# One attention kernel: inner products and values handed to partition groups from SBUF, a new order of the first stages, and the last chunk of keys computed with the values

## The chip, the cores and the metric

The kernel runs on one core of a Trainium2 chip. The metric is the device time in microseconds of one execution. Three executions of the kernel before took 497.56, 498.48 and 500.09 us; their median is 498.48 us. One more execution was profiled: it took 498.01 us, of which the traced span is 496.2 us.

## The reference, cut to what matters

For each of 8 batches, 112 queries of 320 channels (20 heads of 16) attend to 375 tokens of 512 numbers. The last 4 tokens are image prompts, the other 371 are text. Everything is float32.

```python
q   = heads(x @ W_q)                     # 20 heads of 16
k_t = heads(text @ W_k); v_t = heads(text @ W_v)
probs_t  = softmax(q @ k_t.T * D**-0.5)
text_out = probs_t @ v_t
k_ip = heads(ip @ W_k_ip); v_ip = heads(ip @ W_v_ip)
qsem = l2norm(probs_t @ text)            # per head, over 512 numbers
sem  = qsem @ l2norm(ip).T
probs_ip = softmax(q @ k_ip.T * D**-0.5 + 0.5 * sem) * mask
out = (text_out + probs_ip @ v_ip) @ W_out + b_out + x
```

The norm of `qsem` is p G p' for a row p of probabilities, where G holds the inner products of all tokens with each other. So the kernel multiplies the probabilities by G and not by the tokens: one product with the 371 x 371 matrix (only its upper half, doubled off the diagonal), the 4 prompt columns, a column of ones (the softmax's sum) and the head's 16 value columns gives everything that a head needs.

## The kernel before, in words

**Tiling.** Tokens are cut into three chunks of 128 (NT = 3) and into twelve blocks of 32 (BLK = 12, four blocks q to a chunk). Embedding channels are four chunks of 128. The 320 channels of queries and keys are two full chunks and a last one of 64, which is spread over 128 partitions with zeros between the heads (`spread`, L116), so that each head of a group stands at the start of 32 partitions. Heads are handled in five groups g of four heads a; head a of a group uses partitions 32a to 32a+31, and TensorE's four row groups work on four heads.

**Work per batch b.** `transposed_context` (L331) brings the tokens into `ctxT` with the embedding on partitions. `gram` (L352) makes the inner products, and ScalarE and GpSimd write them, doubled off the diagonal, to `ug`. `gram_to_dram` (L374) writes `ug` to the DRAM tile `ud`, and `gram_to_groups` (L378) reads it into `u`, once for each of the four partition groups a, so that token block q of every chunk lies on the 32 partitions of each a. `values` (L403) makes the values in `vext`; `values_to_dram` (L419) and `values_to_groups` (L425) take them through `vd` into `vr` in the same manner. `placed` (L441) copies 16 columns of a head from `vr` into `u` on GpSimd before each group. `keys` (L388) makes the keys `kT`, `project_queries` (L269) the queries of two batches at a time.

**Work per group.** `scores` (L467) makes a head's 112 x 371 scores; `probabilities` (L485) takes the negative row maximum on VectorE (`nmx`), the exponential on ScalarE (`p`), and sends p by one transfer a head on SP's queue into `xg`. `transposed` (L500) is one VectorE transpose of 32 x 32 blocks for the whole group, `xg` to `xgT`. `multiplied` (L510) is the product of `xgT` with `u`, twelve blocks j times four heads. `reduced` (L533) copies the value part (`pvs`) and multiplies and sums the rest with p (`junk`, `ss`). `finish` (L551) computes the prompt attention from these sums and the output product `ps_o`.

**What sets the order.** TensorE, SyncE and VectorE run the order of the source (`manual_schedule`, L89); in the first stages, up to `prologue.close()` (L742), all engines do. The main loop (L744) goes over 40 steps (b, g). In a step, the scores of the step two later are emitted after blocks j = 0 (heads 0 and 1) and j = 4 (heads 2 and 3), and the VectorE transpose of the next step after j = 2. After a step, `between` (L665) places the next batch's preparation: inner products after g = 0, two chunks of values after g = 1, the last chunk and the first keys after g = 2, the other two chunks of keys after g = 3, and after g = 4 the transposes of the context of the batch after it and, for every other batch, the query projection in one piece. SP issues transfers in the order of the source and stops at one whose data is not ready[...].

**Buffers.** PSUM has four banks for products (`ps_qd`), two for scores (`ps_sc`, also used as spares) and two for the rest (`ps_mm`); `bank` (L80) hands out the latter two kinds.

Of the kernel before, what the change touches and what calls it, by code (L numbers as in the profile page):

```python
# [14 lines left out]
NIP = 4  # L15
# [5 lines left out]
def kernel(  # L21
# [26 lines left out]
    CP = NC * P  # L48
    RG = 32
# [12 lines left out]
    OFF = [QN * sum(WC[:c]) for c in range(NT)]  # L62
    UCOL = QN * sum(WC)
    GCOL = [sum(UV - k * P for k in range(c)) for c in range(NT + 1)]
# [32 lines left out]
    wv_sb = const.tile([P, NE, C], F32, tag="wv_sb", name="wv_sb")  # L97
# [8 lines left out]
    FULL = C // P  # L106
    REST = C - FULL * P

# [26 lines left out]
    nc.scalar.dma_start(x_sb[:, 0, :], x[0])  # L135
    load_channels(nc.scalar, wq_sb, w_q)
# [3 lines left out]
    load_embed(nc.sync, wv_in, w_v)  # L140
    load_embed(nc.sync, wk_sb, w_k)

# [23 lines left out]
    for c in range(NT):  # L166
        nc.gpsimd.memset(ug[:, GCOL[c + 1] - 1 : GCOL[c + 1]], 1.0)

# [11 lines left out]

    def more_constants():
        nc.gpsimd.memset(wo_sb[REST:, FULL, :], 0.0)
        for at in attn_ring:
            nc.gpsimd.memset(at[:, C:], 0.0)
# [6 lines left out]
    def order_values():  # L191

        wv_by = wv_sb.rearrange("p e (a g d) -> p e a g d", g=NG, d=D)
        for i in range(FULL):
            nc.vector.tensor_copy(
                wv_by[:, :, :, 2 * i : 2 * i + 2, :],
                wv_in[:, :, i * P : (i + 1) * P].rearrange("p e (a r d) -> p e a r d", r=2, d=D),
            )
        nc.vector.tensor_copy(
            wv_by[:, :, :, 2 * FULL, :],  # L200
            wv_in[:, :, FULL * P :].rearrange("p e (a d) -> p e a d", d=D),
        )
# [29 lines left out]
    def prompt_projections():  # L232

        for i in range(NC):
            ps = bank(f"ps_kip{i}")
            for e in range(NE):
                nc.tensor.matmul(  # L237
                    ps[:, :N],
                    wkip_sb[:, e, i * P : (i + 1) * P],
                    ipT[:, e, :],  # L240
                    start=(e == 0),
                    stop=(e == NE - 1),
                )
            kip = work.tile([P, N], F32, tag="kip", name=f"kip_{i}")
            nc.scalar.copy(kip, ps[:, :N])
            nc.vector.tensor_tensor(
                kipb[:, i],
                kip.rearrange("p (b n) -> p b n", n=NIP).unsqueeze(2).to_broadcast([P, B, HC, NIP]),
                hmask.unsqueeze(1).unsqueeze(3).to_broadcast([P, B, HC, NIP]),
                ALU.mult,  # L250
            )
            yield
# [16 lines left out]
    def project_queries(bs):  # L269
# [7 lines left out]
        for i in range(NC):  # L277
            cn = min(P, C - i * P)
            ps = bank(f"ps_x_{bs[0]}_{i}", spare=bs[0] > 1 and i == 0)
# [31 lines left out]
    def begin(b):  # L311
# [4 lines left out]
        s["ud"] = dram.tile([P, GCOL[NT]], F32, tag="ud", name=f"ud_{b}")  # L316
        s["vext"] = work.tile([P, NT, GROUP, NG, D], F32, tag="vext", name=f"vext_{b}", bufs=1)
        s["vd"] = dram.tile([TP, C], F32, tag="vd", name=f"vd_{b}")
# [7 lines left out]
    def region(b, c):  # L326

        w = WC[c]
        return st[b]["u"][:, OFF[c] : OFF[c] + QN * w].rearrange("p (q w) -> p q w", w=w)

# [20 lines left out]

    def gram(b):  # L352
# [4 lines left out]
        for c in range(NT):  # L357
            t0 = c * P
            k = min(P, TT - t0)
# [9 lines left out]
            g = ug[:, GCOL[c] : GCOL[c] + T - t0]  # L369
            nc.scalar.mul(g, ps[:, : T - t0], 2.0)  # L370
            nc.gpsimd.tensor_tensor(g[:, :k], g[:, :k], half[:, :k], ALU.mult)  # L371
            yield

    def gram_to_dram(b, c0=0, c1=NT):  # L374
        cols = slice(GCOL[c0], GCOL[c1])
        nc.sync.dma_start(st[b]["ud"][:, cols], ug[:, cols])

    def gram_to_groups(b, chunks):  # L378

        s = st[b]  # L380
        for c in chunks:
            for a in range(GROUP):
                nc.sync.dma_start(
                    region(b, c)[a * RG : (a + 1) * RG, :, : UV - c * P],
                    s["ud"][:, GCOL[c] : GCOL[c + 1]].rearrange("(q i) t -> i q t", i=RG),
                )

    def keys(b):  # L388
        s = st[b]
        for i in range(NC):  # L390
            ps = bank(f"ps_k_{b}_{i}")
            for e in range(NE):
# [10 lines left out]
    def values(b):  # L403
        s = st[b]
        ctxT, vext = s["ctxT"], s["vext"]
        for c in range(NT):
            ps = bank(f"ps_v_{b}_{c}")
            for e in range(NE):
                nc.tensor.matmul(  # L409
                    ps[:, :C],  # L410
                    ctxT[:, e, c * P : (c + 1) * P],
                    wv_sb[:, e, :],
# [3 lines left out]
            nc.scalar.copy(vext[:, c].rearrange("p a g d -> p (a g d)"), ps[:, :C])  # L416
            yield

    def values_to_dram(b, eng):  # L419
        eng.dma_start(  # L420
            st[b]["vd"].rearrange("(c p) x -> p c x", p=P),
            st[b]["vext"].rearrange("p c a g d -> p c (a g d)"),
        )

    def values_to_groups(b, eng):  # L425
        s = st[b]
        w = NG * D
        for a in range(GROUP):
            eng.dma_start(
                s["vr"][a * RG : (a + 1) * RG].rearrange("p j g d -> p j (g d)"),  # L430
                s["vd"][:, a * w : (a + 1) * w].rearrange("(j i) x -> i j x", i=RG),
            )
# [118 lines left out]
    def finish(b, heads=(0, H), eng=None, late=False):  # L551
# [7 lines left out]
        def sm(name):  # L559
            return small.tile([S, H], F32, tag=name, name=f"{name}_{b}_{h0}", bufs=2)[:, :n]  # L560

        def sm4(name):
            return small.tile([S, H, NIP], F32, tag=name, name=f"{name}_{b}_{h0}", bufs=2)[:, :n]
# [54 lines left out]
        ps = bank(f"ps_a_{b}_{h0}")  # L618
# [13 lines left out]
        for i in range(i0, i1):  # L632
            nc.tensor.matmul(  # L633
                ps[:S, :C], aT[:, i, :], wo_sb[:, i, :], start=(i == 0), stop=(i == NC - 1)
            )
        if h1 < H:
# [28 lines left out]
    def between(b, g):  # L665
# [4 lines left out]
        if g == 0:  # L670
            if b == 0:
                run(("pp",), None)
            if new:
                run(("g", nb), lambda: gram(nb), 3)
            if b > 0:
# [10 lines left out]
        if g == 3:  # L686
            if new:
                run(("k", nb), None, 2)
            if b > 0:
                run(("f", b - 1), None)  # L690
        if g == 4:
            if nb + 1 < B:
                run(("c", nb + 1), lambda: transposed_context(nb + 1), 3)
            if b > 0:
                run(("f", b - 1), None)
        if b == 0 and g in (1, 2) or b > 0 and g == 4:
            for bs in later:
                run(("q", bs[0]), lambda: project_queries(bs), 3 if b == 0 else 6)
# [3 lines left out]
    products = gram(0)  # L702
    next(prompts)
    next(context)
    next(context)
    next(prompts)
    next(context)
    order_values()
    for c in range(NT):
        next(products)  # L710
        gram_to_dram(0, c, c + 1)
    drain(values(0))
    values_to_dram(0, nc.scalar)
    load_embed(nc.sync, wkip_sb, w_k_ip)
    spread(nc.gpsimd, wq_sb)
    spread(nc.gpsimd, wk_sb)
    drain(project_queries(pairs[0]))
    loaded[1] = load_ctx(1)
    run(("k", 0), lambda: keys(0))
    gram_to_groups(0, range(NT))  # L720
    values_to_groups(0, nc.sync)
# [3 lines left out]
    run(("k", 0), None)  # L725
# [3 lines left out]
    transposed(0, 0)  # L729
    run(("k", 0), None)  # L730
    spread(nc.gpsimd, wkip_sb)
# [5 lines left out]
    nc.sync.dma_start(x_sb[:, 5:, :], x[5:].rearrange("b s c -> s b c"))  # L737
    drain(transposed_context(1))
    run(("pp",), prompt_projections, 3)
    placed(0, 0)  # L740
# [3 lines left out]
    for n, (b, g) in enumerate(steps):  # L744
        coming = steps[n + LEAD] if n + LEAD < len(steps) else None
        for j, _ in enumerate(multiplied(b, g)):
            at = {0: (0, 1), 4: (2, 3)}.get(j, ())
# [11 lines left out]
        if new:  # L759
            if g == 1:  # L760
                gram_to_dram(b + 1)
                load_next(b + 2)
            elif g == 2:
                gram_to_groups(b + 1, (0, 1))
            elif g == 3:
                gram_to_groups(b + 1, (2,))
                values_to_dram(b + 1, nc.sync)
# [5 lines left out]
        if g == 3 and new:  # L773
            values_to_groups(b + 1, nc.sync)
# [51 lines left out]
```

## Time and profile before

| | |
|---|---|
| median of three runs | 498.48 us (497.56 to 500.09) |
| profiled execution | 498.01 us, span 496.2 us |
| TensorE matmuls busy | 468.3 us, 94% of the span |
| VectorE busy | 321.1 us, 65% |
| ScalarE busy | 180.1 us, 36% |
| GpSimd busy | 105.9 us, 21% |
| mean granted TensorE clock | 0.972 |
| bytes moved by transfers | 67.24 MB, mean 136 GB/s |

An engine's busy time counts only its own work, not its waits[...]. The chain of work that ended last is followed back from the end: at each step to what released an instruction, or to the instruction ahead of it on its engine. In all views PE is TensorE, PEld its weight loads, DVE VectorE, ACT ScalarE, POOL GpSimd, SP SyncE; SPq is the issue of a transfer on SP's queue. A name such as `u<-ud` reads: written from.

### The profile page before, as it was taken

To read this page: it belongs to the slowest core of one execution; us is meant where nothing else is said; L and a number is where in the kernel's file an instruction comes from. 1 tells how busy PE (TensorE), PEld (TensorE's weight loads), DVE (VectorE), ACT (ScalarE), POOL (GpSimd) and SP (SyncE) were. 2 spreads that over 40 slices of the span, in tenths; PEclk is the share of its full clock that TensorE was granted. 3 is DMA by queue.
4 is the path that set the end of the run, shared out by engine and by line. 5 is a ranking of instruction groups with operands and counts; after the bars stand their busy time and mean duration, and the time that the engine had idled before them with its cause. 6 is when DMAs were issued, how large, how long until landed. Compare 5 with 4: busy or idle time off the path is not lost.

```text
span 496.2 us, 12853 instructions
## 1 busy us (share of the span) xinstructions
PE 468.3 (94%) x5106; PEld 361.8 (73%) x5106; DVE 321.1 (65%) x692; ACT 180.1 (36%) x505; POOL 105.9 (21%) x245
## 2 busy tenths in 40 slices
PE   6999999999999999999999999999999999987963
PEld 3657777788777787788778787788777887766751
DVE  3045456687765775687756776687756776678862
ACT  2253232235334352335324342335324432243232
POOL 4301200002501124012501124012501232011540
PEclk9997999999999999999999999999999999998895
DMA  7588447542595236942595236842595227732300
GB/s 217 157 198 237 100 152 163 156 114 63 154 228 153 58 95 172 210 121 67 163 229 142 67 98 171 199 116 76 171 220 140 67 87 162 195 101 78 101 13 12
DMA packets 61075, 67.24 MB, mean 136 GB/s; under 512 B 22128, under 2 KB 56192, under 8 KB 61016
## 3 DMA queue, kind: packets, MB, share of 16 engines
q1 hardware_dynamic: 60096, 65.32, 50.3%
q10 hardware_dynamic: 920, 1.11, 0.8%
q8 instruction: 40, 0.66, 0.6%
q14 instruction: 19, 0.16, 0.1%
HBM read 31.65 MB, written 8.17 MB: 80 GB/s over the span
## 4 chain that ended last, share of the span: by engine, by line
PE 84%; DVE 5%; ACT 3%; DMA 2%; POOL 2%; issue 2%; SPq 1%; POOLq 0%; ACTq 0%; DVEq 0%
PE ps_qd L523 37%; PE ps_k L393 11%; PE ps_v L409 11%; PE ps_g L362 9%; PE ps_s L476 7%; PE ps_q L289 2%; PE ps_c L339 2%; PE ps_o L633 2%; DVE junk L538 1%; POOL wv L606 1%; DMA vr<-vd 1%; DVE qm L298 1%; PE ps_kip L237 1%; PE ps_ip L456 1%; DMA ip_sb<-in_ctx_dram 1%
## 5 line engine op out<-in xcount | busy, mean ns | idle before, releaser
L523 PE MATMUL ps_qd<-u,xgT 32*112 32x296 f32 (+11 forms) x3840 | 244.4, 365 | 3.5 <-POOL u L445 1.4
L523 PEld LDWEIGHTS ps_qd<-u,xgT 32*112 32x112 f32 x3840 | 196.8, 174 | 33.6 <-issue 7.3
L493 ACT ACTIVATE p<-ps_s,nmx 112x371 f32<-112x371 f32 x160 | 82.3, 568 | 159.8 <-DVE nmx L489 141.6
L489 DVE TENSOR_REDUCE nmx<-ps_s 112x1 f32<-112x371 f32 x160 | 77.4, 528 | 76.0 <-PE ps_s L476 74.7
L504 DVE STREAM_TRANSPOSE xgT<-xg 128x1536 f32<-128x1536 f32 x40 | 118.9, 2971 | 5.2 <-DMA xg<-p 5.2
L538 DVE CUSTOM_DVE_ANT_0 junk<-ps_qd,p 112x371 f32<-112x371 f32 x160 | 87.1, 544 | 45.3 <-ACT pvs L536 28.0
L476 PE MATMUL ps_s<-kT,qm 32*112 32x371 f32 x320 | 75.0, 496 | 2.8 <-ACT p L493 2.2
L445 POOL COPY u<-vr 128x64 f32<-128x64 f32 x120 | 26.6, 238 | 224.8 <-PE ps_qd L523 161.5
L393 PE MATMUL ps_k<-ctxT,wk_sb 128*128 128x371 f32 x192 | 63.6, 480 | 0.0
L409 PE MATMUL ps_v<-wv_sb,ctxT 128*128 128x320 f32 x192 | 55.6, 440 | 0.0
L393 PEld LDWEIGHTS ps_k<-ctxT,wk_sb 128*128 128x128 f32 x192 | 35.7, 190 | 21.7 <-issue 1.1
L476 PEld LDWEIGHTS ps_s<-kT,qm 32*112 32x112 f32 x320 | 36.8, 173 | 15.8 <-ACT kT L400 3.2
L362 PE MATMUL ps_g<-ctxT 128*128 128x375 f32 (+2 forms) x192 | 45.3, 394 | 0.7 <-issue 0.7
L409 PEld LDWEIGHTS ps_v<-wv_sb,ctxT 128*128 128x128 f32 x192 | 35.2, 190 | 13.5
L362 PEld LDWEIGHTS ps_g<-ctxT 128*128 128x128 f32 x192 | 33.4, 197 | 12.3 <-issue 3.8
L400 ACT COPY kT<-ps_k 128x371 f32<-128x371 f32 x24 | 11.3, 469 | 41.4 <-PE ps_k L393 41.3
L606 POOL TENSOR_TENSOR wv<-vip,w 112x1280 f32<-112x1280 f32 (+1 forms) x8 | 19.2, 2404 | 31.8 <-DVE w L604 31.8
L298 DVE TENSOR_SCALAR qm<-ps_q,emask 128x224 f32<-128x224 f32 (+1 forms) x25 | 9.2, 400 | 24.2 <-PE ps_q L289 24.0
L416 ACT COPY vext<-ps_v 128x320 f32<-128x320 f32 x24 | 10.2, 427 | 33.5 <-PE ps_v L409 33.5
L371 POOL TENSOR_TENSOR ug<-ug,half 128x128 f32<-128x128 f32 (+1 forms) x24 | 11.3, 472 | 41.6 <-ACT ug L370 41.6
L536 ACT COPY pvs<-ps_qd 112x21 f32<-112x21 f32 x160 | 16.5, 200 | 6.9 <-PE ps_qd L523 6.9
L289 PE MATMUL ps_q<-xT,wq_sb 128*128 128x224 f32 (+1 forms) x90 | 16.8, 332 | 1.9 <-ACT xT L284 0.9
(95 smaller groups left out, 272.4 us busy)
## 6 DMA issues: line engine op xcount, KB each, us to landing
xg<-p SPq DMA_DIRECT2D x160, 162.3 KB
u<-ud SPq DMA_DIRECT2D x32, 188.0 KB
vip<-vipd SPq DMA_DIRECT2D x8, 560.0 KB
ct<-in_ctx_dram SPq DMA_DIRECT2D x16, 256.0 KB
u<-ud SPq DMA_DIRECT2D x32, 124.0 KB
vr<-vd SPq DMA_DIRECT2D x32, 120.0 KB
vd<-vext SPq DMA_DIRECT2D x7, 480.0 KB
ud<-ug SPq DMA_DIRECT2D x7, 372.0 KB
```

The source lines that it names most:

```text
L289: nc.tensor.matmul(ps[:, : n * S], wq_sb[:, j, i * P : (i + 1) * P], xT[:, j, : n * S], start=(j == 0), stop=(j == NC - 1),)
L362: nc.tensor.matmul(ps[:, : T - t0], ctxT[:, e, t0 : t0 + P], ctxT[:, e, t0:T], start=(e == 0), stop=(e == NE - 1),)
L393: nc.tensor.matmul(ps[:, :TT], wk_sb[:, e, i * P : (i + 1) * P], s["ctxT"][:, e, :TT], start=(e == 0), stop=(e == NE - 1),)
L409: nc.tensor.matmul(ps[:, :C], ctxT[:, e, c * P : (c + 1) * P], wv_sb[:, e, :], start=(e == 0), stop=(e == NE - 1),)
L445: nc.gpsimd.tensor_copy(region(b, c)[:, :, UV - c * P :], s["vr"][:, c * QN : (c + 1) * QN, g, :])
L476: nc.tensor.matmul(ps[:S, :TT], qm[a * RG : (a + 1) * RG, i, r, j * S : (j + 1) * S], s["kT"][a * RG : (a + 1) * RG, i, :], start=True, st ...
L489: nc.vector.tensor_reduce(nmx, ps[:S, :TT], AX.X, ALU.max, negate=True)
L493: nc.scalar.activation(p, ps[:S, :TT], AF.Exp, bias=nmx)
L504: nc.vector.transpose(xT.rearrange("p j (k q) -> p q j k", q=QN), xg.rearrange("p q (j k) -> p q j k", k=RG),)
L523: nc.tensor.matmul(banks[a][:S, j * RG : UW], xT[a * RG : (a + 1) * RG, j, :S], region(b, c)[a * RG : (a + 1) * RG, q, q * RG :], start=(j ...
L538: nc.vector.tensor_tensor_reduce(out=junk, in0=ps[:S, :TT], in1=s["p", g][:, a, :], scale=1.0, scalar=0.0, op0=ALU.mult, op1=ALU.add, accu ...
L606: eng.tensor_tensor(wv, s["vip"][:, :, part], w.rearrange("p h n -> p n h").unsqueeze(3).to_broadcast([S, NIP, n, D]), ALU.mult,)
```

## The change

**First stages.** The queries' input and weights and the second batch's context are loaded on SP's queue right behind the values' weights. Four products of the identity with itself are put ahead of everything (`awake`). The first batch's inner products are made block by block as soon as a chunk of context is transposed (`first_gram`). One chunk of values, the transposes of the queries' input and the other chunks of values follow; the projections of queries stand between the first chunk of keys and the scores; the other two chunks of keys follow the scores of two groups. The prompts' keys and values are projected together after the first group and the second batch's inner products.

**Transfers.** `u` is laid out by token block, and so are the rows of `ug`, with 16 columns of zeros at the end of each chunk. `gram_to_groups` copies 32 rows of `ug` to `u`, for each of four blocks and four partition groups, SBUF to SBUF: 16 transfers a batch, 8 after g = 1 and 8 after g = 2. `values_to_groups` does the same with `vext` and `vr`: 8 transfers after g = 2 behind the last chunk of values, 8 after g = 3. `ud` and `vd` are gone.

**Keys.** From the second batch on, the weights of the last 64 key channels stand behind the values' weights, so a chunk of values has 384 columns. GpSimd copies the key part to `k3` with zeros between heads, and three transposes make the last chunk of keys from it.

**Order between groups.** Scores of heads 2 and 3 come after block j = 6, but in the last batch. The three transposes of a query projection go after g = 3 between the last two chunks of keys, the projections after g = 4 around a last part of the output product, which `finish` now yields before. The context of the batch after next is loaded after g = 0. `ps_a` and two of three `ps_x` use score banks. Small tiles of `finish` have one buffer and not two.

```diff
@@ loads
-    nc.scalar.dma_start(x_sb[:, 0, :], x[0])
-    load_channels(nc.scalar, wq_sb, w_q)
     load_embed(nc.sync, wv_in, w_v)
+    nc.sync.dma_start(x_sb[:, 0, :], x[0])
+    load_channels(nc.sync, wq_sb, w_q)
     load_embed(nc.sync, wk_sb, w_k)
+    loaded[1] = load_ctx(1)
@@ region
-        return st[b]["u"][:, OFF[c] : OFF[c] + QN * w].rearrange("p (q w) -> p q w", w=w)
+        u = st[b]["u"].rearrange("p (q w) -> p q w", w=GW)
+        return u[:, :, GCOL[c] : GCOL[c + 1]]
@@ new
+    def awake(n):
+        ps = bank(f"ps_w_{n}", spare=True)
+        for _ in range(n):
+            nc.tensor.matmul(ps[:, :P], ident, ident, start=True, stop=True)
+    def first_gram():
+        ctxT = st[0]["ctxT"]
+        banks = []
+        for c in range(NT):
+            banks.append(ps_qd.tile([P, 512], F32, tag="qd", name=f"ps_g_0_{c}"))
...
+            c0, c1 = c * P, min(c * P + P, T)
+            for r in range(c + 1):
+                for e in range(NE):
+                    nc.tensor.matmul(banks[r][:, c0 - r * P : c1 - r * P],
+                        ctxT[:, e, r * P : (r + 1) * P], ctxT[:, e, c0:c1], ...)
+                if c == NT - 1:
+                    doubled(banks[r], r)
+                yield
@@ gram_to_groups
-                    region(b, c)[a * RG : (a + 1) * RG, :, : UV - c * P],
-                    s["ud"][:, GCOL[c] : GCOL[c + 1]].rearrange("(q i) t -> i q t", i=RG),
+                    st[b]["u"][a * RG : (a + 1) * RG, q * GW : (q + 1) * GW],
+                    ug[q * RG : (q + 1) * RG, :],
@@ keys
+            if b > 0 and i == FULL:
+                for c in range(NT):
+                    rows = min(P, TT - c * P)
+                    nc.tensor.transpose(ps[:, c * P : c * P + rows],
+                        s["k3"][:rows, c].rearrange("p a r d -> p (a r d)"), ident[:rows, :rows])
+                nc.scalar.copy(s["kT"][:, i, :], ps[:, :TT])
@@ values
+        w = C if b == 0 else C + REST
...
+            if b > 0 and c == NT - 1:
+                nc.gpsimd.tensor_copy(s["k3"][:, :, :, 0, :],
+                    vext[:, :, C:].rearrange("p c (a d) -> p c a d", d=D))
@@ values_to_groups
+        for q in blocks:
+            for a in range(GROUP):
+                nc.sync.dma_start(by_block[a * RG : (a + 1) * RG, q],
+                    s["vext"][q * RG : (q + 1) * RG, :, a * w : (a + 1) * w])
@@ finish
-        ps = bank(f"ps_a_{b}_{h0}")
+        ps = bank(f"ps_a_{b}_{h0}", spare=b < B - 1)
...
+            if h1 - h0 == H and i == 1:
+                yield
@@ between, g == 3 and g == 4
-                run(("k", nb), None, 2)
+                run(("k", nb), None, 1)
+            for bs in later if b > 0 else ():
+                run(("q", bs[0]), lambda: project_queries(bs), 3)
+            if new:
+                run(("k", nb), None, 1)
...
+                run(("f", b - 1), None, 1)
+            for bs in later if b > 0 else ():
+                run(("q", bs[0]), lambda: project_queries(bs), 2)
+            if b > 0:
                 run(("f", b - 1), None)
+            for bs in later if b > 0 else ():
+                run(("q", bs[0]), lambda: project_queries(bs), 1)
@@ first stages
-    drain(values(0))
-    values_to_dram(0, nc.scalar)
...
-    drain(project_queries(pairs[0]))
-    loaded[1] = load_ctx(1)
+    drain(products)
+    gram_to_groups(0, range(QN))
+    run(("v", 0), lambda: values(0))
+    run(("q", 0), lambda: project_queries(pairs[0]), 3)
+    run(("v", 0), None, 2)
+    values_to_groups(0, (0, 1))
...
+    run(("q", 0), None)
     run(("k", 0), lambda: keys(0))
+    run(("q", 0), None)
...
+    run(("q", 0), None)
+    values_to_groups(0, (2, 3))
...
-    run(("pp",), prompt_projections, 3)
@@ main loop
-            at = {0: (0, 1), 4: (2, 3)}.get(j, ())
+            at = {0: (0, 1), 6 if b < B - 1 else 4: (2, 3)}.get(j, ())
...
-            if g == 1:
-                gram_to_dram(b + 1)
+            if g == 0:
                 load_next(b + 2)
+            elif g == 1:
+                gram_to_groups(b + 1, (0, 1))
             elif g == 2:
-                gram_to_groups(b + 1, (0, 1))
+                gram_to_groups(b + 1, (2, 3))
             elif g == 3:
-                gram_to_groups(b + 1, (2,))
-                values_to_dram(b + 1, nc.sync)
+                values_to_groups(b + 1, (2, 3))
...
-        if g == 3 and new:
-            values_to_groups(b + 1, nc.sync)
+        if g == 2 and new:
+            values_to_groups(b + 1, (0, 1))
```

## The prediction

> **What bounds the kernel now.** I began with the page's busy table and its chain: matmuls fill TensorE for 94% of the span, and 84% of the chain that ended last is TensorE. Time taken off its instructions, or off a wait between them, is time off the end; work elsewhere counts only where TensorE stands still for it.
>
> ```profile
> PE 468.3 (94%) x5106; PEld 361.8 (73%) x5106; DVE 321.1 (65%) x692; ACT 180.1 (36%) x505; POOL 105.9 (21%) x245
> ...
> PE 84%; DVE 5%; ACT 3%; DMA 2%; POOL 2%; issue 2%; SPq 1%; POOLq 0%; ACTq 0%; DVEq 0%
> ```
>
> Busy time hides short waits, since ends of matmuls are modelled. So I went through the chain in order of time. In one batch the chunk of values and the chunk of keys stand there at their real cost:
>
> ```profile
> 77.45 2.35 PE ps_v L409 x8
> 79.80 2.49 PE ps_k L393 x8
> ```
>
> Between two groups of heads where queries are projected, the chain leaves TensorE:
>
> ```profile
> 267.16 1.42 PE ps_c L339 x12
> 268.58 1.62 PE ps_o L633 x6
> 270.19 0.21 PE ps_x L281 x2
> ...
> 270.43 0.60 ACT xT L284 x2
> ...
> 271.07 1.42 PE ps_q L289 x6
> ...
> 272.51 0.82 DVE qm L298 x2
> ...
> 273.36 0.35 ACT qT L301
> ...
> 273.75 1.40 PE ps_q L289 x6
> ```
>
> TensorE stood from 270.40 to 271.07 and from 272.49 to 273.75, 1.93 us, waiting for a PSUM bank. Elsewhere from 60 to 430 us the chain stays on TensorE, but for the last 11 us. Third, the start: the first weighted product stands at 44.20 us, at half the clock (windows of 2 us; columns are matmul busy time, granted clock, DMA share, GB/s):
>
> ```profile
> 40.00:42.00 2.00, 2.00 (x19) 0.93 0.66 192
> 42.00:44.00 2.00, 1.42 (x7) 0.50 0.74 183
> 44.00:46.00 2.00, 1.80 (x12) 0.50 0.79 252
> 46.00:48.00 2.00, 2.00 (x16) 0.50 1.08 340
> ```
>
> Last, the queue of SP, which the change loads (timeline of one batch):
>
> ```profile
> 247.43 3.81 SPq L383 DMA_DIRECT2D u<-ud  x8
> ...
> 263.45 1.85 SPq L429 DMA_DIRECT2D vr<-vd  x4
> ```
>
> A transfer of 32 partitions takes SP 0.475 us to issue; one of xg<-p takes 0.80 (median of its 160).
>
> [...] weight loads of the first 375-column product are 0.62 us apart (10.55, 11.18, 11.80)[...], until 14.3 us; later chunks run at twice that. [...] transposes from 3.7 to 8.5 us brought no fast clock, and the half clock from 42 us follows transposes and 32-column products. [...] 2.49 us for 8x371 is 0.311 each[...]. [...] here the write of vd takes 2.82 us and the reading back 4.35.
>
> **The change, part by part.**
>
> *Keys.* For seven of eight batches the last chunk loses its eight matmuls, 2.49 us. Values get 64 columns more in 24 matmuls[...]. Three transposes come in at 1.42/12 = 0.118 us: 0.35. Net -0.86, times 7: **-6.0**. The copy to k3 on POOL (0.2 to 0.6 us, like u<-vr and ug) stands about ten us ahead of its transposes; ACT's wider copy of vext adds 0.04. Both are covered by TensorE's next group; without that cover, under 1 us a batch.
>
> *Queries.* The input transposes go one step earlier, between the two last chunks of keys; the output product is split so that its last part stands between the second and third projection. By the chain, the waits of three such stages are 1.92 (159 us), 1.93 and 1.41: 5.3. In the new order the bank that the third projection needs is drained under 1.42 + 0.54 us of other matmuls, against 1.17 of draining. ps_a now takes a score bank: 0.1 to 0.2 us may be lost behind ACT's copies. **-4.9**. The first pair (83 us) keeps its 1.24.
>
> *Scores at block 6.* They are emitted later by two blocks, about 1 us. But the maxima of heads 2 and 3 stand behind VectorE's transpose of 2.97 us, which ends later than either place. I take 0; bounds -0.1 to +0.1 a step, 33 steps, -3 to +3.
>
> *Transfers.* Per batch, 12 u + 4 vr + one ud + one vd become 16 + 16 from SBUF. SP: 32 x 0.475 + 20 x 0.80 + some six others = 34 us of 53 to 58. Worst place, counted from the end of group 2's products: the last p transfer ends at 2.1, eight u at 5.9, vip 6.3, eight vr at 10.1. Heads 0 and 1 of the next p, ready from 7.6, wait behind them until 10.1; but heads 2 and 3, ready at 11.7 and 12.3, then go 0.3 late, and only the last counts for the transpose. That starts some 2.5 us into a group, takes 3.0, and is needed 5.9 + 3.0 us after the group's start (its products and the shortest work between groups), so 3.4 us are to spare. Cost 0. The wait of POOL for vr (63.3 us in 7 places) vanishes; it touches TensorE only at 437 us: **-0.3**. The 16 waits on separate u transfers in a batch's first group cost about nothing: 12 such stand there now, and that group takes 6.07 us in the chain (217.06 to 223.13) against 5.86 for the next (228.40 to 234.26).
>
> *Start.* The inner products start as soon as the first chunk is transposed, but with the same 741 columns, cold. Counting half-clock durations (1.7 us per 128-column block of four) from 5.8 us, with the clock rising at 14.3 as now, they end at 16.2, against 17.1. [...] From there: values 6.5, transposes 0.4, query 0.85, keys 2.5, query 0.85 bring the first scores at +11.1 (now +13.75). Exponentials after a 1.28 us table load: +13.9 to +15.4. On SP four p transfers reach +17.1, eight vr +20.9; landing takes 2.4 (now: eight take 7.29 us from 35.15, so four end at 38.8, and the transpose starts at 41.2), placing 0.25: first product at +23.5, 39.7 us (now 44.2). [...] I keep the half clock: 7.5 us for the group. Then inner products 5.3, the prompts' keys 2.7 (three times 0.9, now ahead of 44.2), values 2.3: group 1 at 57.5 against 59.5: **-2.0**. Bounds: with a clock that rises by 9 us and stays, -8; with no rise before 18 us and transfers landing 2 us later, +2.
>
> Sum: -6.0 - 4.9 - 0.3 - 2.0 = -13.2. The profiled execution took 498.01 (span 496.2), so 484.8; the median of the runs is 0.47 above it: **485.3 us**.
>
> **Rivals.**
> 1. *The start gains more*: [...] 5 to 6 us more, about 479. For: TensorE is busy from 1.4 us. Against: half of that is transposes.
> 2. *Only matmul work is saved*: the new transfer order gives back the start, and the bank waits return in another place (score banks are now shared by ps_x, ps_a, ps_c and ps_o): -6 alone, 492.
> 3. *SP becomes the bound, and the kernel slower.* The place is the sixteen issues after group 2. With an issue time of t, the next group's four p transfers land at 8.1 + 16t; TensorE waits when this passes about 20.2 (needed at 16.9, 3.4 to spare), so from t = 0.76 us. Each further 0.1 costs 1.6 us in seven batches. The gain of 13.2, 1.9 a batch, is gone at 0.88; at the 1.03 that twelve u issues took in the first stage (12.39 us at 20.65[...]), 515. For: that figure[...]. Against: steady stages show 0.475 for eight in a row with longer reads.
> 4. *Parts cancel*: within 0.5%.
>
> **How the numbers follow.** My case (480 to 491) 0.58; rival 1 (475 to 480) 0.16; rival 2 (491 to 496) 0.15; rival 4 0.04; rival 3 0.07. A difference of 0.5%, 2.5 us, is about what the runs (497.56 to 500.09) can tell from none. Faster 0.89, same 0.04, slower 0.07. The range 476 to 494 leaves out about 0.2: the far ends of rivals 1 and 2, and rivals 3 and 4 whole.
>
> **What would show it.** Keys: 17 whole chunks of ps_k, 136 matmuls where 192 stood, beside 21 transposes; ps_v at 128x384, 2.7 to 2.8 us a chunk. Queries: no DVE qm or ACT qT in the chain after 100 us. Start: first product near 40 us, group 1 near 57.5. SP: issues of u and vr below 0.6 us each after group 2, and no DVE xgT waiting for xg<-p. I am wrong if VectorE's transpose waits in every batch, if ACT or DVE stands in the chain at the score matmuls, or if the clock view shows half rate outside start and end.

## The result and the profile after

Four executions of the changed kernel took 521.12 to 526.99 us, median 525.28. Runs of the kernel before beside them had a median of 498.51 us. The ratio is 1.054 with a 95% interval of 1.049 to 1.060: the change costs 27 us where a gain of 13 was forecast. The profiled execution has a span of 525.0 us, 28.8 more than before.

The page of the changed kernel, its busy table, TensorE's clock in 40 slices and the shares of the chain:

```profile
PE 472.6 (90%) x5103; PEld 358.8 (68%) x5103; DVE 321.9 (61%) x692; ACT 180.0 (34%) x505; POOL 109.4 (21%) x257
...
PEclk9998999989997999979997999979998999988885
...
PE 77%; DVE 5%; DMA 5%; issue 5%; ACT 4%; POOL 2%; SPq 1%; POOLq 0%; DVEq 0%; ACTq 0%
```

TensorE stands still more (90% busy, was 94%), and yet its busy time is longer, 472.6 us against 468.3: the clock row, all nines before from 50 to 445 us, now has a 7 or an 8 in nearly every batch. In the chain DMA went from 2% to 5% and "issue" (time in which an engine waits for nothing that is shown) from 2% to 5%. What TensorE waits for is told by its waits from 113 to 411 us, five whole batches (engine, line, releaser: total, times, longest):

```profile
PE ps_c L350 <- ACT p L547: 16.8, 5, 4.0
PE ps_k L435 <- ACT xT L296: 0.4, 1, 0.4
```

One wait a batch, always at the third transpose chunk of the coming context (`ps_c`, after group 4), which takes a spare score bank, and always for an exponential. The chain through one such place, in order of time:

```profile
153.03 1.04 ACT p L547 x2
154.07 0.19 SPq L550
...
154.35 3.13 DMA xg<-p
...
157.61 0.12 DVE xgT L558
157.74 2.61 issue
160.34 0.49 DVE nmx L543
160.84 0.02 issue
160.86 0.58 ACT p L547
161.44 0.04 issue
161.48 1.03 PE ps_c L350 x4
162.51 2.13 PE ps_o L687 x4
164.64 3.70 PE ps_q L301 x12
168.34 0.54 PE ps_o L687 x2
168.88 1.14 PE ps_q L301 x6
170.02 0.86 PE ps_qd L577 x8
```

The last p transfer of group 3 is issued at 154.3 and lands at 157.5. The two exponentials at 153.03, to which the chain leads further back, are not what held it: they belong to the next group, whose p goes out from 160.51. The four transfers issued from 150.84 had their exponentials at 143.10 and 146.72 us, two heads each, so p was ready at 147.75 and waited for SP. Only when it has landed can VectorE transpose (the 2.61 us of "issue" are that transpose, 157.61 to 160.49). The maxima of heads 2 and 3 stand behind it in VectorE's order, the exponentials behind the maxima; until these have read the scores, no score bank is free for `ps_c`. TensorE stood from 157.6 to 161.48. After it, `ps_o` takes 2.13 us for four matmuls and `ps_q` 3.70 for twelve; without a wait ahead of them they take 1.08 and 2.27 (last chain of the experiments). The clock by windows (busy time of PE, PEld, DVE, ACT, POOL; granted clock; DMA share; GB/s):

```profile
156.00:160.00 4.00, 1.60 (x28) 1.31 (x22) 2.39 (x1) 0.00 (x0) 0.00 (x0) 1.00 0.33 80
160.00:164.00 4.00, 2.52 (x8) 1.84 (x9) 2.92 (x9) 2.75 (x9) 0.59 (x3) 0.57 0.40 104
164.00:168.00 4.00, 4.00 (x14) 3.48 (x13) 1.36 (x4) 0.24 (x1) 0.00 (x0) 0.57 0.27 78
```

Why p is late shows on SP's queue (start, duration, transfers):

```profile
138.13 6.35 SPq L422 DMA_DIRECT2D u<-ug  x8
144.53 0.59 SPq L490 DMA_DIRECT2D vip<-vipd  x1
145.22 5.51 SPq L483 DMA_DIRECT2D vr<-vext  x8
150.84 4.32 SPq L550 DMA_DIRECT2D xg<-p  x4
155.21 5.21 SPq L483 DMA_DIRECT2D vr<-vext  x8
```

From 138.13 to 150.73 SP issues the sixteen transfers and vip without a pause, and p stands behind them. I had counted 8.0 us for this stretch; it takes 12.6. From one batch's inner products to the next, batches 2 to 7, it was 57.9, 53.1, 57.9, 53.1 and 56.3 us before; now it is 62.5, 58.3, 61.3, 58.0 and 58.1.

### The profile page after: what moved, and what is told of

It reads as the page before. It is cut to its first block, busy times and chain, and to the rows that moved or that the text cites. A ratio compares the mean times of both kernels' runs of the same rounds, so it can differ in the third digit from the quotient of the medians.

```text
span 525.0 us, 13008 instructions
## 1 busy us (share of the span) xinstructions
PE 472.6 (90%) x5103; PEld 358.8 (68%) x5103; DVE 321.9 (61%) x692; ACT 180.0 (34%) x505; POOL 109.4 (21%) x257
## 4 chain that ended last, share of the span: by engine, by line
PE 77%; DVE 5%; DMA 5%; issue 5%; ACT 4%; POOL 2%; SPq 1%; POOLq 0%; DVEq 0%; ACTq 0%
PE ps_qd L577 31%; PE ps_v L461 12%; PE ps_k L444 8%; PE ps_g L408 7%; PE ps_s L530 6%; DMA xg<-p 5%; PE ps_o L687 4%; PE ps_q L301 3%; ACT p L547 2%; PE ps_c L350 1%; DVE nmx L543 1%; DVE junk L592 1%; PE ps_g L380 1%; SPq L483 1%; POOL wv L660 1%
## 5 line engine op out<-in xcount | busy, mean ns | idle before, releaser
L577 PE MATMUL ps_qd<-u,xgT 32*112 32x40 f32 (+11 forms) x3840 | 242.8, 368 | 9.7 <-POOL u L499 8.1
L577 PEld LDWEIGHTS ps_qd<-u,xgT 32*112 32x112 f32 x3840 | 195.1, 175 | 44.5 <-issue 8.7
L543 DVE TENSOR_REDUCE nmx<-ps_s 112x1 f32<-112x371 f32 x160 | 77.4, 527 | 66.3 <-PE ps_s L530 58.3
L461 PE MATMUL ps_v<-wv_sb,ctxT 128*128 128x384 f32 (+1 forms) x192 | 64.7, 487 | 0.0
L444 PE MATMUL ps_k<-ctxT,wk_sb 128*128 128x371 f32 x136 | 45.9, 482 | 0.0
L408 PE MATMUL ps_g<-ctxT 128*128 128x375 f32 (+2 forms) x168 | 37.4, 379 | 0.0
L444 PEld LDWEIGHTS ps_k<-ctxT,wk_sb 128*128 128x128 f32 x136 | 25.1, 190 | 15.4 <-issue 0.5
L350 PE MATMUL ps_c<-ident,ct 128*128 128x128 f32 (+1 forms) x96 | 16.9, 319 | 18.2 <-ACT p L547 17.6
L687 PE MATMUL ps_o<-wo_sb,aT 128*112 128x320 f32 x48 | 25.1, 672 | 6.0 <-ACT p L547 5.2
L350 PEld LDWEIGHTS ps_c<-ident,ct 128*128 128x128 f32 (+1 forms) x96 | 12.1, 163 | 21.3 <-ACT p L547 19.0
L468 ACT COPY vext<-ps_v 128x384 f32<-128x384 f32 (+1 forms) x24 | 11.3, 472 | 39.0 <-PE ps_v L461 30.3
L301 PEld LDWEIGHTS ps_q<-xT,wq_sb 128*128 128x128 f32 x90 | 17.5, 220 | 4.1 <-issue 1.8
```

The source lines that it names most:

```text
L301: nc.tensor.matmul(ps[:, : n * S], wq_sb[:, j, i * P : (i + 1) * P], xT[:, j, : n * S], start=(j == 0), stop=(j == NC - 1),)
L350: nc.tensor.transpose(ps[:, e * P : e * P + rows], ct[:rows, c, e * P : (e + 1) * P], ident[:rows, :rows],)
L408: nc.tensor.matmul(ps[:, : T - t0], ctxT[:, e, t0 : t0 + P], ctxT[:, e, t0:T], start=(e == 0), stop=(e == NE - 1),)
L444: nc.tensor.matmul(ps[:, :TT], wk_sb[:, e, i * P : (i + 1) * P], s["ctxT"][:, e, :TT], start=(e == 0), stop=(e == NE - 1),)
L461: nc.tensor.matmul(ps[:, :w], ctxT[:, e, c * P : (c + 1) * P], wv_sb[:, e, :w], start=(e == 0), stop=(e == NE - 1),)
L543: nc.vector.tensor_reduce(nmx, ps[:S, :TT], AX.X, ALU.max, negate=True)
```

## The experiments

Theory Q came out of this reading: the eight `vr` issues after group 2 hold back p on SP's queue, and so the transpose, the maxima and the score banks. Rivals: B, the score banks that `ps_c`, `ps_x`, `ps_a` and `ps_o` now share are too few by themselves; S, the later scores of two heads; L, transfers from SBUF to SBUF are slow to land, whoever issues them and when.

### Which transfers, and where they stand

Values of batches 1 to 7 through DRAM again; the products the same way; both; and all transfers kept, but eight moved behind p.

```diff
 # values through DRAM (e1)
             elif g == 3:
-                values_to_groups(b + 1, (2, 3))
+                values_to_dram(b + 1)
...
-        if g == 2 and new:
-            values_to_groups(b + 1, (0, 1))
+        if g == 3 and new:
+            values_from_dram(b + 1)
 # products through DRAM (e2); e3 has both edits
             elif g == 1:
-                gram_to_groups(b + 1, (0, 1))
+                gram_to_dram(b + 1)
             elif g == 2:
-                gram_to_groups(b + 1, (2, 3))
+                gram_from_dram(b + 1, (0, 1))
             elif g == 3:
+                gram_from_dram(b + 1, (2,))
 # eight issues moved (e6), in the loop over blocks
-        if g == 2 and new:
-            values_to_groups(b + 1, (0, 1))
+            if j == 7 and g == 3 and b + 1 < B:
+                values_to_groups(b + 1, (0, 1))
```

> The changed kernel, with the values of batches 1 to 7 written to DRAM after group 3 and read back by four transfers, as before the change; the products still go straight from SBUF. Theory Q (SP's queue: eight issues of vr after group 2, 5.5 us, hold back the four p transfers of group 3, so VectorE's transpose in group 4 starts late, the maxima of heads 2 and 3 stand behind it, their score banks stay full and TensorE waits): most of the loss goes, 488 to 496 us, and TensorE no longer waits for an exponential ahead of the third ps_c in group 4. Theory B (score banks shared by ps_c, ps_x, ps_a and ps_o are themselves too few) and theory S (two heads' scores at block 6): 520 to 526, nothing of that moves. Theory L (transfers between SBUF and SBUF land late, whoever issues them): 505 to 515, as half of them go.

> The changed kernel, with the inner products of batches 1 to 7 through DRAM (one write, twelve reads, placed as before the change); the values go straight from SBUF. Theory Q: eight u issues after group 2 take some 3.8 instead of 5.9 us, the eight of vr stay, so p goes out 2 us earlier of some 6 that it is late: 508 to 516. Theories B and S: 520 to 526. Theory L: 505 to 515.

> The changed kernel with both ways through DRAM for batches 1 to 7; the first batch's transfers, the new first stages, the last chunk of keys behind the values, the split query stage, the shared score banks and the scores at block 6 stay. Theory Q: the whole loss goes and the other parts' gain of 11 to 13 us shows, 485 to 489. Theories B and S: still above 515. Theory L: 485 to 489 as well.

> The changed kernel with every transfer kept, but the eight issues of vr for blocks 0 and 1 moved on SP from the end of group 2 to block 7 of group 3, behind that group's four p transfers. Theory Q: the transposes of group 4 start in time; the sixteen vr issues now stand ahead of group 4's p transfers, which have a longer group to land in: 490 to 505. Theories B and S: 520 to 526. Theory L, and SP being short of time as a whole: 518 to 526.

| kernel | median us | ratio to before | 95% interval |
|---|---|---|---|
| values through DRAM | 489.57 | 0.983 | 0.978 to 0.988 |
| products through DRAM | 521.99 | 1.049 | 1.043 to 1.054 |
| both through DRAM | 494.71 | 0.991 | 0.988 to 0.994 |
| eight `vr` issues behind p | 507.74 | 1.021 | 1.015 to 1.028 |

Taking the values' transfers away takes 36 us away and makes the kernel faster than before. TensorE's waits of that kernel from 110 to 380 us, five batches, are these:

```profile
PE ps_k L436 <- ACT xT L296: 0.4, 1, 0.4
PE ps_q L301 <- ACT qT L313: 0.3, 1, 0.3
```

B and S fall as causes by themselves: shared banks and late scores are all in there. The products' transfers matter little (3 us, the intervals overlap, and 508 to 516 was expected): the eight `vr` still stand ahead of p and here take 7.04 us and not 5.51, so that p is issued from 149.97, counted from the inner products only 1.1 us earlier than in the changed kernel. L falls as the main cause with the moved issues: the same 32 transfers, and 17.5 us less (just outside the 490 to 505 expected). There TensorE no longer waits for an exponential from 113 to 400 us; what is left stands at another place, the first placing of a batch's values on POOL, for which sixteen `vr` issues in a row (11.31 us) and group 4's p come late (the profile puts POOL's own wait down to transfers of p, the last ones issued; I did not separate the two). TensorE's waits for it in the whole trace, 5.3 us of them ahead of the first product:

```profile
PE ps_qd L577 <- POOL u L499: 21.4, 6, 5.3
```

Both through DRAM was a miss: 5 us above the values alone, where all was to be gained. Its four reads of `ud`, at the end of group 3, stand ahead of the write of `vd` (149.53 against 146.80 us); SP then waits for that write before it can issue the reads of `vr` (until 154.03), and p of group 4 stands behind. That this costs the 5 us is not shown: the traced run is the fastest of ten (491.62 us), and over five batches it is only 1.9 us behind the values alone.

### One part alone, and the order on VectorE

```diff
 # the kernel before with the transfers alone (e4)
-                gram_to_groups(b + 1, (0, 1))
+                products_sbuf(b + 1, (2, 3))
...
+        if g == 2 and new:
+            values_sbuf(b + 1, (0, 1))
 # scores of heads 2 and 3 at block 4 (e5)
-            at = {0: (0, 1), 6 if b < B - 1 else 4: (2, 3)}.get(j, ())
+            at = {0: (0, 1), 4: (2, 3)}.get(j, ())
 # transpose behind the maxima in group 4 (e7)
-            if j == 2 and n + 1 < len(steps):
+            if j == (7 if g == 4 and b < B - 1 else 2) and n + 1 < len(steps):
```

> The kernel before with one part of the change alone: the products and values of batches 1 to 7 go to the partition groups straight from SBUF, 16 and 16 transfers at the places that the changed kernel gives them (with the load of a context one group earlier, as there). First stages, keys, queries, bank sharing and scores at block 4 are those of before. Theory Q (the eight vr issues after group 2 hold back p): the loss comes with the transfers alone. The changed kernel lost 35.7 us against its version with values through DRAM; here 520 to 540 us. If the loss needed the scores at block 6 or the shared banks too, less: 500 to 510; if it lay in those parts alone, 497 to 501.

> The changed kernel with the scores of heads 2 and 3 at block 4 in all batches, everything else kept. Theory Q: p still stands behind the vr issues; the two heads' maxima run before the late transpose only if their scores come before it, and with the scores at block 4 they are still behind it in VectorE's order, as the transpose is issued at block 2: 520 to 526. Theory S: below 505.

> The changed kernel with every transfer where it is, but VectorE's transpose in group 4 of a batch issued at block 7, behind the maxima of heads 2 and 3, instead of at block 2. It tells two forms of theory Q apart. Form M (what costs is that the maxima and so the exponentials and score banks stand behind the waiting transpose): TensorE goes on to ps_c, ps_o and ps_q during the wait, and the next group starts some 5 us earlier in six batches: 490 to 502. Form X (what costs is that the next group's products need the late transpose itself): 517 to 527.

The transfers alone cost the kernel before 2.6% (510.27 us; ratio 1.026, interval 1.017 to 1.036), a third of what I expected from theory Q, and at the edge of the 500 to 510 that I had set for a loss that needs another part of the change as well. The mechanism is there, but smaller. TensorE's waits in five batches of it:

```profile
PE ps_c L340 <- ACT p L514: 5.2, 5, 1.4
PE ps_q L290 <- ACT xT L285: 0.9, 3, 0.3
```

Same place and same releaser, 1.0 us a batch where the changed kernel has 3.4. And no window of that stage is at half clock: `ps_o` takes 1.72 us for six matmuls, where the changed kernel has 3.20. So the loss is not in proportion to the wait. Two things make the wait shorter. In the five batches p's last transfer lands 42.0 to 42.4 us after the inner products began, in the changed kernel 42.8 to 44.4, 1.4 later on average; in the first of them, 2.3 us later, one long issue of `u` makes 1.3 of it (8 take 5.03 us here, 6.35 there), whose cause I did not find. And TensorE is ready for the third `ps_c` 45.1 to 45.4 us after the inner products began, in the changed kernel at 43.8 to 44.5: the work that the change saves brings it to the wait 1.0 us sooner. Together that is about the difference of 2.3 us; no effect of the shared banks is needed for it.

With the scores at block 4 the changed kernel takes 520.37 us (ratio to before 1.044, interval 1.036 to 1.052, which overlaps that of the change): S is no cause of its own. At most it adds some 5 us to Q, and over the five batches the two traces differ by 0.3 us.

The later transpose told form M from form X only in part: 516.64 us (1.038, interval 1.030 to 1.047), just below X's 517 to 527 and far from M's 490 to 502. The maxima no longer wait for p, and TensorE goes on to `ps_c`. But then the sums of group 4 stand behind the transpose, and behind them the queries' masks. The chain there:

```profile
157.69 2.76 issue
160.45 0.54 DVE junk L592
...
163.09 0.73 DVE qm L310 x2
...
163.85 0.35 ACT qT L313
...
164.25 1.77 PE ps_q L301 x6
166.02 1.59 PE ps_qd L577 x8
```

In the two of the five batches without a projection of queries TensorE waits for `u` from POOL instead, 2.4 and 2.8 us. So VectorE had no slack behind the transpose to give: in both orders tried TensorE waits for something when p is late.

### The half clock, and what lands ahead of p

```diff
 # sixteen idle products between the second and third ps_c (e10)
-                run(("c", nb + 1), lambda: transposed_context(nb + 1), 3)
+                run(("c", nb + 1), lambda: transposed_context(nb + 1), 2)
+                dummies(b, 16)
+                run(("c", nb + 1), None, 1)
 # values in halves behind p (e11)
+            if j == 7 and g == 3 and b + 1 < B:
+                values_to_groups(b + 1, (0, 1))
+            if j == 7 and g == 4 and b + 1 < B:
+                values_to_groups(b + 1, (2, 3))
```

> The changed kernel with sixteen matmuls of 128 columns on the identity (some 1.7 us, their result unused) between the second and the third ps_c of group 4, where TensorE stands 3.9 us for an exponential. Nothing is shortened in SP's queue or on VectorE. It separates the wait itself from the half clock after it: there ps_c, ps_o and ps_q take 1.03, 2.13 and 3.70 us instead of about 0.6, 1.1 and 2.3, some 2.8 us a batch. If the shorter idle keeps the clock up: 507 to 513. If the clock falls all the same, or the loss is the wait alone: 524 to 529.

> The changed kernel with all transfers from SBUF kept, but vr for blocks 0 and 1 issued at block 7 of group 3 and for blocks 2 and 3 at block 7 of group 4, each eight behind that group's four p transfers. Theory Q: no p stands behind a vr any more; against the order with all sixteen at block 7 of group 3 (507.7 us), the batches that lost 2 us there gain it: 490 to 500. The risk is that the second half lands after group 4 and POOL's placing is late: 500 to 512, with TensorE waiting for u from POOL. If the transfers' number and not their place counts: 505 to 510.

The dummies were a failed design: 544.78 us (1.093). Their bank came free only behind an ACT copy (160.65 us) that itself waits for the late exponentials (159.33), so they ran after the gap, of 4.34 us there, and not in it. That shows the half clock all the same (the chain there):

```profile
161.19 6.30 PE ps_w L372 x32
167.49 0.40 PE ps_c L350 x4
167.89 1.08 PE ps_o L692 x4
168.97 2.27 PE ps_q L301 x12
171.24 0.54 PE ps_o L692 x2
171.78 1.14 PE ps_q L301 x6
172.91 0.86 PE ps_qd L582 x8
```

The dummies took the slow stretch upon themselves (6.30 us, and not the 1.7 that I had reckoned). The real work behind them runs at full rate in 5.42 us (167.49 to 172.91), in the changed kernel in 8.54 (161.48 to 170.02). The half clock costs 3.1 us here, almost as much as the wait of 3.9. Over five batches: the changed kernel is 28.6 us behind the one with values through DRAM (298.1 against 269.6 from the inner products of batch 2 to those of batch 7), of which 16.8 are waits; the other 11.8, or 2.4 a batch, agree with that: TensorE works 25.6 us at half clock there, which loses 12.8.

The half clock comes in pieces of one length. In the clock records of all fourteen traces, a stretch at half rate that begins between 90 and 440 us lasts 3.4, 6.8 or 10.2 us, and within one trace the starts lie whole multiples of 3.41 us apart; in the changed kernel they are 3.4 us from 106.0, 6.8 from 160.6, 222.0, 280.1 and 341.5, and 3.4 from 399.5. All 24 waits of 2.87 us or more in this part of the traces have such a stretch. Of the 31 shorter ones from 0.7 us on, 12 have: one of 0.77 us has (at 103.08 in the changed kernel), one of 1.36 (the kernel before with the transfers alone) and one of 2.85 (products through DRAM) have not. So what a wait costs beyond itself depends in part on where it falls in these pieces.

Values in halves cost far more than I allowed for, 539.39 us (1.082, interval 1.076 to 1.088). Issued at block 7 of group 4 they land too late for the first placing; in its trace, of the longest of its five runs (545.96 us), TensorE waits 46.2 us in 9 places for `u` from POOL. Over the five batches these waits are 24.8 of the 37.9 us by which it is behind the kernel with values through DRAM; 27.9 us of work at half clock lose the rest. So the transfers from SBUF had no good place among those tried on this queue: ahead of p they delay the transpose, behind it the values. Another engine's queue was not tried.

Two runs took the kernel with values through DRAM further: scores at block 4 again, and the values' write one group earlier. The second was meant to take away SP's wait between write and reads; then vip, the largest transfer in that stretch, was moved behind p as well.

```diff
 # write of the values behind group 2, reads at the end of group 3 (e8)
             elif g == 3:
-                values_to_dram(b + 1)
+                values_from_dram(b + 1)
...
-        if g == 3 and new:
-            values_from_dram(b + 1)
+        if g == 2 and new:
+            values_to_dram(b + 1)
 # and the prompts' values behind p (e13)
-        if g == 2:
+        if g == (4 if new else 2):
             prompt_values(b)
```

> The kernel with the values of batches 1 to 7 through DRAM (489.6 us), where TensorE has no wait in the steady batches, with the scores of heads 2 and 3 at block 4 instead of 6. It prices the later scores where SP's queue is not late. Counted at nothing in the prediction (bounds -3 to +3): 487 to 493. If the later scores cost by making p later: below 487; if they help: above 493.

> The kernel with the values of batches 1 to 7 through DRAM (489.6 us), with the write issued one group earlier, behind group 2's products, and the four reads at the end of group 3. There SP stood 3.4 us between the write and the reads (issue at 146.80, the reads at 150.73), with group 4's p transfers behind it. Theory Q: that wait goes: 484 to 488. If group 4's p transfers had time to spare: 489 to 490.

> The kernel with the values' write issued behind group 2's products (494.8 us), with the prompts' values vip (560 KB) fetched in group 4 instead of group 2 for batches 0 to 6, so behind group 4's p transfers. In that kernel the last p transfer of group 3 landed 5.46 us after its issue (148.38 to 153.84), behind 480 KB of vd and 560 KB of vip; in the changed kernel 3.13. Theory Q with landing as its second half (what is issued ahead of p delays it in the DMA engines too): p lands about 1.5 to 2 us earlier, TensorE's waits of 3.8 us at ps_c go: 487 to 491. If only SP's issues count: 494 to 496.

With scores at block 4: 493.38 us (0.993, interval 0.991 to 0.995), against 0.983 (0.978 to 0.988) at block 6. Where p is in time, the later scores gain some 4 us. The traces show it in the scores themselves: counted from the start of each matmul to the start of the next, TensorE spends 12.2 us on them in five batches at block 4, 8.7 at block 6. Why they are cheaper there stays open.

The early write alone made it slower, 494.77 us (0.993). SP issues the four p of group 3 no more slowly (3.75 us, and 4.18 with the write in its old place), but p lands later:

```profile
148.38 5.46 DMA xg<-p
```

5.46 us from issue to landing, where the changed kernel shows 3.13 at this place: 480 KB of `vd` and 560 KB of vip were issued ahead of it. TensorE's waits for exponentials at `ps_c` and `ps_o` came back, 5.0 us in all. With vip behind p they are gone again, and the kernel takes **488.65 us**, ratio 0.978 (interval 0.975 to 0.982), the fastest of all and faster than before; the values through DRAM with vip in its old place are as fast within the spread (0.978 to 0.988). The stage of the long chain above, in this kernel:

```profile
157.48 1.42 PE ps_c L351 x12
158.90 1.08 PE ps_o L702 x4
159.98 2.27 PE ps_q L301 x12
162.25 0.54 PE ps_o L702 x2
162.79 1.14 PE ps_q L301 x6
163.92 0.86 PE ps_qd L592 x8
```

All of it is TensorE, without a gap and at full rate. VectorE's transpose starts 40.2 us after the batch's inner products began; in the changed kernel it was 44.5. Those 4.3 us stand there as TensorE's wait of 3.9.

## Why the prediction was wrong, by its own steps

**The step that failed is "Transfers": "so 3.4 us are to spare ... Cost 0".** Two of its numbers were off. The issue of a transfer from SBUF was taken over from the row for transfers from DRAM, 0.475 us; the sixteen measure 0.59 at the median, and with the gaps between them and one long issue 0.74 (6.35 + 5.51 for sixteen). With that the formula of rival 3, 8.1 + 16t, puts the landing at 19.9, still just inside its bound of 20.2; the real one is 21.8 after group 2's products (135.7 to 157.5); 1.1 of the rest is that p's own four issues took 4.32 us and not 3.2. And the bound itself was wrong. I asked who needs `xgT` and found the next group's products. I did not ask what else stands behind the waiting transpose on VectorE, though I had written, under the scores, that the maxima of heads 2 and 3 do. They hold the score banks that `ps_c` needs, at 157.6; counted back over transpose, maximum and exponential (161.44 - 157.5 = 3.9 us), p had to land by 153.7, that is 18.0 and not 20.2. With both put right, rival 3 decides at t = 0.62 and not 0.76. It had a chance of 0.07.

**The price of a wait.** Rival 3 counted a late microsecond as a lost microsecond. All five waits, of 2.5 to 4.0 us, had a stretch at half clock behind them as well, which cost 2.4 us a batch on top of 3.4 of waiting.

**Keys: right.** Chain of the changed kernel:

```profile
77.25 2.78 PE ps_v L461 x8
80.02 2.49 PE ps_k L444 x8
...
92.01 2.69 PE ps_k L444 x8
94.70 0.32 PE ps_k L435 x3
```

A chunk of values went from 2.35 to 2.78 us, forecast 2.7 to 2.8; the last chunk of keys from 2.49 to 0.32, forecast 0.35. From a chunk of keys, 2.49 us for 8 x 371 columns, 64 more columns in 24 matmuls are reckoned at 1.29 us a batch (an estimate); measured are 3 x 0.43. 3 x 0.43 + 0.32 - 2.49 = -0.88 a batch; forecast -0.86.

**Queries: the mechanism was right, the size wrong.** The forecast took 1.93 us of standing TensorE a stage from the chain, 270.40 to 271.07 and 272.49 to 273.75. TensorE's own timeline of that stage in the kernel before shows less:

```profile
270.03 0.74 PE L281 MATMUL ps_x<-ident,x_sb 112*128 112x112 f32 x6
271.07 4.09 PE L289 MATMUL ps_q<-xT,wq_sb 128*128 128x224 f32 x18 [0.30 <-ACT xT L284]
```

While the chain is on `qm` and `qT`, the second projection runs, from 272.50 to 273.60; TensorE stands 0.30 us ahead of the first projection and 0.15 ahead of the third. In the kernel with values through DRAM `ps_q` and `ps_x` of the three stages take 2.0 us less than before, not 4.9. And `qm` and `qT` are not all gone from the chain: in the fastest kernel they stand there once after 100 us, at 376.18.

**Scores at block 6: not nothing.** Counted at 0, bounds -3 to +3; with p in time they gain some 4 us, and with p late they cost up to 5, which the intervals do not settle.

**The sum of these three agrees by luck.** Five batches of the kernel with values through DRAM take 269.6 us, before 278.4. That is -8.8, and the steps give nearly that, 5 x 0.86 for keys and 4.9 for three query stages, 9.2. But counted from matmul to matmul it is -4.3 for keys and values, -2.0 for the queries, -3.9 for the scores, and +1.3 for the rest.

**Start: right in part.** In this trace the clock rose at 7.0 us (the start of its first record at full rate; 14.4 in the kernel before) and the inner products end at 13.23, where I had 16.2; that is on rival 1's side. But it is luck, and what the four products with the identity did to it is not shown. Twelve traces of this record have the same first stages: in eight the clock rose at 4.7 to 8.0 us and these products ended at 12.3 to 13.6, in four, the fastest kernel's among them, it rose at 12.2 to 13.6 and they ended at 15.5 to 16.2. And SP lost the gain again. Sixteen `u` take 11.00 us from 14.07 where 16 x 0.475 is 7.6, and the last `vr` issue ends at 39.36. The first product stands at 41.11 (forecast 39.7), at half clock (recorded from 37.7 to 44.5), which I had kept there as an estimate; group 1 stands at 58.68 (forecast 57.5, before 59.53): -0.9 and not -2.0.

**Values' wait of POOL: wrong, and small.** TensorE waits 8.1 us for `u` from POOL, where it waited 1.4 before; 6.1 of the 8.1 stand ahead of the first product.

What the text named as signs of error showed: the transpose waits for p in six batches (2.8 to 4.8 us), the clock view has half rate inside, and the issues are at 0.59 just within "below 0.6", so that the median alone would have passed.

What stays open is why a few issues take 1.3 to 2.2 us in some kernels. A wait of SP for the transfer eight places ahead on its queue does not fit: in the changed kernel's trace nothing of that transfer lands while such an issue lasts; at the one of 1.90 us from 142.58 it had landed by 140.41.

## What to carry to other kernels

Count a queue's work with the issue time of the transfer that will stand there, and for every instruction that may come late ask for everything behind it on its engine and which buffers that work holds, not only who reads its result. A transfer that saves bytes is dear if it multiplies issues ahead of a short one on the critical loop: 1 + 4 transfers through DRAM beat 16 straight from SBUF here by 36 us. And price a wait of TensorE with the clock that it may lose: here all 24 waits of 2.87 us or more, from 90 to 440 us, lost some, and 12 of the 31 shorter ones.

## What the runs showed of the hardware

- An issue on SP takes 0.59 us for a transfer of 32 partitions from SBUF to SBUF, in the kernel before 0.43 to 0.47 for one from DRAM, 0.40 to 0.53 for the write of all values to DRAM (medians; single issues took up to 2.2); 1 or 3 KB a partition made no difference (`vr` 0.60, `u` 0.59).
- TensorE's clock was at half in stretches of 3.4, 6.8 or 10.2 us (all those that begin between 90 and 440 us in the fourteen traces). Behind waits of 2.5 to 4.0 us `ps_o` took 2.05 to 2.13 us for four matmuls, against 1.08; behind waits of 0.9 to 1.4 us at the same place (the kernel before with the transfers alone) the rate stayed full. A stretch also stood behind shorter waits, down to one of 0.77 us. The five in the changed kernel stand among transposes: between the last matmul ahead and the first behind that is no transpose 4.4 to 5.9 us pass there. What decides whether a wait is followed by a stretch was not shown.
- What is issued ahead of a transfer can delay its landing: p took 3.1 to 3.8 us from issue to landing in six batches of the changed kernel, with eight small transfers ahead, and 4.7 to 5.5 in four of five batches with 1,040 KB ahead; with 560 KB of these moved behind it, TensorE's waits were gone. The bytes are not all of it: with the scores at block 4 and the same small transfers ahead it took up to 4.8.
